# A planned two-layer cross-attention stack: the values in column quarters and 32-row strips, no transposing transfers, the last stage by pairs

## The chip, the cores and the metric

The kernel runs on one core of one Trainium2 chip. The core has five engines with queues of their own: TensorE (PE in the profile; its weight loads stand apart as PEld), VectorE (DVE), ScalarE (ACT), GpSimd (POOL) and SyncE (SP), which here only issues transfers. The metric is the device time of one execution in microseconds; the time before is the median of three runs.

## The reference, cut to what matters

x has 2 x 1024 rows of 256; the context has 2 x 77 rows of 256; 16 heads of 16 features. Four residual stages follow each other, each behind a layer norm:

```python
x = x + tanh(g_xattn[0]) * xattn0(layernorm(x), ctx, ...)        # 16 heads, softmax over 77 keys
x = x + tanh(g_ffn[0])  * ffn0(layernorm(x), w1, w2)             # 256 -> 1024 gelu -> 256
x = x + tanh(g_xattn[1]) * xattn1(layernorm(x), ctx, dist, ...)  # softmax(q k + distance bias), biases
x = x + tanh(g_ffn[1])  * ffn1(layernorm(x), ...)                # expert 0 alone: 256 -> 1024 relu -> 256,
                                                                 # residual, layer norm, gamma, beta
# ffn0, both linears: weights rounded to -1, 0, 1 times their mean magnitude;
# activations rounded to whole numbers of at most 127 in magnitude, by row
```

## The kernel before, in words

The 2048 rows are 16 tiles of 128 rows, in four groups of G = 4. A group runs through four stages: attention of layer 0, `bit_ffn`, attention of layer 1, `expert_ffn`. Nothing is looped on the chip: every step is added to a `Plan` with the tiles that it reads and writes, a cost in microseconds and one or more engines that may do it. `Plan.order` is a list scheduler: of the steps that are ready it takes, engine by engine, the one that can begin first, ties by a weight; buffers of a pool count as resources. `Plan.best` runs it PASSES + 1 times, with weights from the longest path plus `OFFSET[stage][group]` at first and from a backward pass later, and keeps the order with the earliest planned end. `issue` writes it out, so each engine's queue is that order.

**PSUM.** Eight banks: four are the one buffer of scores, `sc` (L711); four are the pool "b" that `bank` hands out for all else. A stage-3 step leaves LEAVE = 2 of them free.

**Attention** (`attention`, L676 on). `norm_group` takes the statistics of the group (`stats`, L517/L518), `inverse_std` makes rstd on POOL (L529, L530) and shift on DVE (L535), and xn = x * rstd + shift is made tile by tile (L553). `transposed_group` turns xn on PE (L581) and evicts it (L371, the line of all evictions by ACT). Queries: L694. Scores: L718, four heads' rows of 32 in four products abreast, 154 keys of two heads each. The softmax of a tile of 128 rows and 8 heads (616 columns) goes: eviction (layer 0, ACT L371) or addition of the distance bias (layer 1, DVE L757); maximum (DVE L766); subtraction (L771); exp (ACT L778); sum (DVE L782) and reciprocal (L787); multiplication (L791). Subtraction and multiplication may go to POOL or DVE; in the order as planned all 64 of each are POOL's. There are 64 such tiles: 2 layers, 4 groups, 2 halves of heads, 4 tiles.

**Values** (`values`, L797 on): for a group and a half of the heads the 616 columns are cut at 128 into five pieces, each turned by four PE transposes (L810) and evicted to pT. A piece crosses heads, so the values stand in `vbd` as blocks of 32 columns (two heads), one for each pair of a piece and a column quarter (`PIECES`, eight of them); `weighted` (L823) runs the eight products of 512 columns in the order of `ORDER`, so that four column quarters run abreast. One eviction brings the sums to OT, and L844 makes the output product.

**bit_ffn** (L978 on). xn is scaled and rounded by adding ROUND (L984), ROUND is taken off again with a bf16 result (`unround`, L963), and a transposing transfer on SP's queue (`turned`, L975) makes xqT. L1007 is the first product, L1015 gelu, then the same rounding (L1023), `unround` to hq, transposing transfer to hqT, second product L1036.

**expert_ffn** (L1053 on). L1071 and L1089 are its two products in f32; L1099 adds the residual, `stats` of all four tiles follow, one `inverse_std`, then gamma and scaling by tile (L1108, L1115), and one store for each tile (L1122).

Transfers are issued from SP in the order of the plan; the four weights of layer 0's attention from ACT.

## Time and profile before

| | us |
|---|---|
| median of 3 runs (385.62 to 386.3) | 385.67 |
| the profiled execution | 384.3 |
| its span, first to last instruction | 382.6 |
| PE busy | 331.5 |
| DVE busy | 279.4 |
| ACT busy | 248.8 |
| POOL busy | 230.9 |

The mean granted TensorE clock was 0.958. The profile's page gives busy sums, the span in 40 slices (each digit a busy share in tenths), the chain of work that ended last, and groups of instructions by line. A busy sum counts a moment once even where instructions overlap; the "mean ns" of a group is the length of one record, which on a pipelined engine can be longer than the spacing of two. A product of f32 operands shows as two records, an f32 transpose as one.

### The profile page before, as it was taken

Reading aid. Unit: us, or ns where it says so; the run is one execution under the profiler, and the core shown is the slowest. Engines: PE = TensorE matmul, PEld = TensorE weight load, DVE = VectorE, ACT = ScalarE, POOL = GpSimd, SP = SyncE. Lnnn points to the kernel's source line nnn. Section 1 sums busy time; section 2 is a strip of 40 time slices with the busy share of each in tenths; the row PEclk is TensorE's granted clock in tenths of the full one; section 3 lists DMA queues with packets and bytes.
Section 4 is the critical chain, followed back from the end, with each engine's and each line's share of the span. In section 5 each row is a group of like instructions: output and inputs, shape, how many; then the busy total and the mean of one; then the engine's idle time right before and its main releaser. Section 6 shows DMA issues by size and latency. Waiting matters only on the chain.

```text
span 382.6 us, 5624 instructions
## 1 busy us (share of the span) xinstructions
PE 331.5 (87%) x1983; PEld 207.2 (54%) x1992; DVE 279.4 (73%) x587; ACT 248.8 (65%) x407; POOL 230.9 (60%) x241
## 2 busy tenths in 40 slices
PE   4883894989758779999899999999999999999991
PEld 3453452446424446644676747446774644785580
DVE  2599889679899997489946899569998994037006
ACT  1797789998788965476629985797556474223300
POOL 6269999631779765489649755313898696025001
PEclk9897998899999788999999999999999999999997
DMA  7972303125011111000100014223000001001001
GB/s 235 337 209 32 110 5 110 32 27 99 1 27 30 28 27 29 0 2 2 29 0 3 0 29 96 69 42 70 2 0 2 1 15 42 0 3 55 0 0 55
DMA packets 39600, 17.73 MB, mean 46 GB/s; under 512 B 30099, under 2 KB 39060, under 8 KB 39572
## 3 DMA queue, kind: packets, MB, share of 16 engines
q1 hardware_dynamic: 38484, 16.33, 16.9%
q10 hardware_dynamic: 1088, 1.05, 0.8%
q8 instruction: 15, 0.25, 0.2%
q14 instruction: 13, 0.11, 0.1%
HBM read 9.71 MB, written 2.10 MB: 31 GB/s over the span
## 4 chain that ended last, share of the span: by engine, by line
PE 45%; DVE 24%; ACT 13%; POOL 9%; issue 4%; DMA 3%; SPq 0%; POOLq 0%; DVEq 0%; ACTq 0%
PE b L1089 10%; PE b L1071 10%; DVE mx L766 5%; PE b L810 5%; PE b L823 5%; PE b L844 5%; POOL probs L791 4%; DVE den L782 4%; PE b L694 4%; DVE probs L757 3%; ACT pT L371 3%; PE b L1036 2%; POOL probs L771 2%; PE sc L718 2%; ACT probs L778 2%
## 5 line engine op out<-in xcount | busy, mean ns | idle before, releaser
L771 POOL TENSOR_TENSOR probs<-probs,mx 128x616 f32<-128x616 f32 x64 | 78.1, 1235 | 34.1 <-DVE mx L766 34.1
L791 POOL TENSOR_TENSOR probs<-probs,den 128x616 f32<-128x616 f32 x64 | 80.9, 1286 | 5.2 <-DVE den L787 4.2
L810 PE MATMUL b<-ident,probs 128*128 128x128 f32 (+1 forms) x320 | 50.1, 300 | 21.7 <-POOL probs L791 9.9
L1089 PE MATMUL b<-staged,hT 128*128 128x256 f32 x256 | 59.2, 382 | 0.0
L1071 PE MATMUL b<-xnT,staged 128*128 128x512 f32 x128 | 57.5, 597 | 0.3 <-ACT xnT L371 0.3
L810 PEld LDWEIGHTS b<-ident,probs 128*128 128x128 f32 (+1 forms) x320 | 37.5, 148 | 37.3 <-POOL probs L791 13.8
L766 DVE TENSOR_REDUCE mx<-probs 128x8 f32<-128x616 f32 x64 | 48.8, 784 | 6.3 <-ACT probs L371 5.7
L1089 PEld LDWEIGHTS b<-staged,hT 128*128 128x128 f32 x256 | 47.5, 190 | 9.4 <-issue 3.4
L778 ACT ACTIVATE probs<-probs 128x616 f32<-128x616 f32 x64 | 44.9, 715 | 11.6 <-POOL probs L771 11.3
L782 DVE TENSOR_REDUCE den<-probs 128x8 f32<-128x616 f32 x64 | 48.8, 767 | 4.6 <-ACT probs L778 4.6
L371 ACT ACTIVATE pT<-b 128x512 f32<-128x512 f32 (+1 forms) x80 | 42.7, 603 | 9.0 <-PE b L810 8.3
L553 ACT ACTIVATE xn<-x,shift,rstd 128x256 f32<-128x256 f32 x64 | 34.0, 595 | 19.4 <-DVE shift L535 19.4
L529 POOL TENSOR_SCALAR rstd<-mv 128x4 f32<-128x4 f32 x20 | 5.4, 268 | 64.0 <-DVE mv L518 63.9
L1071 PEld LDWEIGHTS b<-xnT,staged 128*128 128x128 f32 x128 | 23.5, 190 | 27.1 <-issue 24.7
L371 ACT ACTIVATE hT<-b,eb_sb 128x512 f32<-128x512 f32 x32 | 21.9, 684 | 23.3 <-PE b L1071 23.3
L694 PE MATMUL b<-xnT,wq_sb 128*128 128x512 f32 x64 | 32.8, 634 | 1.2 <-ACT xnT L371 1.2
L823 PE MATMUL b<-pT,vbd 128*32 128x512 f32 (+1 forms) x256 | 31.9, 599 | 1.5 <-ACT pT L371 1.3
L844 PE MATMUL b<-wo_sb,OT 128*128 128x256 f32 x128 | 29.9, 382 | 0.4 <-ACT OT L371 0.3
L517 DVE BATCH_NORM_STATS2 st<-x 128x6 f32<-128x256 f32 x64 | 24.7, 417 | 6.8 <-DMA x<-in_x_dram 5.9
L718 PE MATMUL sc<-kbd,qT 32*128 32x154 f32 x512 | 27.6, 325 | 2.0 <-DVE probs L757 1.3
L718 PEld LDWEIGHTS sc<-kbd,qT 32*128 32x128 f32 x512 | 19.1, 189 | 17.4 <-issue 6.1
L941 DVE TENSOR_REDUCE top_h<-hs 128x1 f32<-128x1024 f32 x16 | 19.3, 1204 | 11.1 <-ACT hs L1015 11.1
(87 smaller groups left out, 491.1 us busy)
## 6 DMA issues: line engine op xcount, KB each, us to landing
x<-in_x_dram SPq DMA_DIRECT2D x16, 128.0 KB
staged<-in_ew_dram SPq DMA_DIRECT2D x2, 1024.0 KB
out_dram<-x SPq DMA_DIRECT2D x16, 128.0 KB
staged<-in_fw1T_dram SPq DMA_DIRECT2D x1, 1024.0 KB
staged<-in_fw2T_dram SPq DMA_DIRECT2D x1, 1024.0 KB
dbias<-in_dist_dram SPq DMA_DIRECT2D x1, 616.0 KB
wk_sb<-in_wkT_dram ACTq DMA_DIRECT2D x1, 256.0 KB
wq_sb<-in_wqT_dram ACTq DMA_DIRECT2D x1, 256.0 KB
```

What stands on the lines that cost most here:

```text
L371: nc.scalar.activation(out(), src(), AF.Relu if relu else AF.Copy if bias is None else AF.Identity, bias=0.0 if bias is None else bias(), ...
L718: nc.tensor.matmul(sc.ap[:, q, j * QK : j * QK + QK], qT.ap[rows, h, at : at + P], kbd.ap[rows, h, b].rearrange("p h s -> p (h s)"), start ...
L766: lambda j, n: nc.vector.tensor_reduce(each(mx, j, n), heads(j, n), AX.X, ALU.max),
L771: lambda e, j, n: e.tensor_tensor(heads(j, n), heads(j, n), bc(each(mx, j, n), 2, SK), ALU.subtract),
L778: lambda j, n: nc.scalar.activation(flat(j, n), flat(j, n), AF.Exp), [pr], [pr],
L782: lambda j, n: nc.vector.tensor_reduce(each(den, j, n), heads(j, n), AX.X, ALU.add),
L791: lambda e, j, n: e.tensor_tensor(heads(j, n), heads(j, n), bc(each(den, j, n), 2, SK), ALU.mult),
L810: lambda j=j, c=c, n=n, tr=tr: nc.tensor.transpose(tr.ap[:n, j, :], prs[j // 2].ap[:, j % 2, c * P : c * P + n], ident.ap),
L823: nc.tensor.matmul(po.ap[32 * q : 32 * q + 32, :], vbd.ap[: CH[c], b, h, s, :], pTs[c].ap[: CH[c], :], start=(i < 4), stop=(i >= 4),)
L844: nc.tensor.matmul(pp.ap[:, j % 2, :], OT.ap[:, k, j * P : (j + 1) * P], wo_sb.ap[:, k, :], start=(k == 0), stop=(k == KT - 1),)
L1071: lambda f=f, k=k, ph=ph: nc.tensor.matmul(ph.ap, ew1_sb.ap[:, k, f * P : (f + 1) * P], xnT.ap[:, k, :], start=(k == 0), stop=(k == KT - 1),),
L1089: lambda j=j, f=f, pp=pp: nc.tensor.matmul(pp.ap[:, j % 2, :], hT[f].ap[:, j * P : (j + 1) * P], ew2_sb.ap[:, f, :], start=(f == 0), stop= ...
```

## The change

Line numbers below are those of the kernel before.

- **Values.** The last 13 of a head's 77 keys are treated apart. The multiplication by the reciprocal is split in two: keys 61 to 76 of each of the 8 heads go to a new strip of 128 columns behind the 616 (written first), keys 0 to 63 are packed to 8 x 64 columns in place. The five transposed pieces are then four of two whole heads each, and the strip. `chunks(i)` makes, for a pair of tiles i, four products of 128 rows, 32 columns, 256 moving columns, one in each column quarter, into a bank of its own; `strips` adds eight products of 32 rows by 32 columns, 256 moving columns. `vbd` is laid out anew, with zeros against the three keys that the strip repeats. OT is evicted by pairs, and the output product of a pair waits for that pair alone. `strip(q, i)` also permutes which bank of `sc` a product of scores goes to.
- **Layer 0 without xn.** x is transposed as it is; Wq is centred once over its 256 inputs (`center`: two products with a matrix of 1/256, one subtraction), and exp takes rstd as its scale for each row. No shift is made for layer 0.
- **No transposing transfers.** Rounding adds LIFT = 0x4400 as well, so that the low half of each f32 is a bf16 pattern; `turned` transposes these halves (stride 2) on PE with a bf16 identity, and one eviction reads PSUM as 16-bit integers, takes LIFT off and writes bf16. `unround`, xq and hq are gone; hs has three buffers for two.
- **Last stage by pairs.** In `expert_ffn` the second pair's second products wait for the first pair's; statistics, rstd and scaling go by pairs, with no shift, and one store serves a pair. Loads of x, from group 1 on, go by pairs too.
- **Planner.** All 16 entries of OFFSET are new, PASSES is 8 for 6, and costs are formulas of the group's size (GROUPS = (4, 4, 4, 4)).

The diff, cut to its core:

```diff
+LIFT = float(0x4400)
+GROUPS = (4, 4, 4, 4)
 OFFSET = (
-    (-5, -26, -123, -47),
-    (-3, -24, -97, -118),
-    (13, 125, -3, -121),
-    (222, 127, -1, 13),
+    (424, -150, -409, -294),
+    (-2, 172, -151, -389),
+    (319, 8, 80, -221),
+    (40, 177, 231, 300),
 )
-PASSES = 6
+PASSES = 8
...
+    MAIN, LAST = 64, 16
+
+    def strip(q, i):
+        return (q + 2 * i) % 4
...
+        def lay(row, part, own, head):
+            parts.append((vbd, len(parts)))
+            n = own.stop - own.start
+            at = slice(HD * head, HD * head + HD)
+            dma(
+                0.5,
+                lambda: nc.sync.dma_start(
+                    out=vbd.ap[row : row + n, part].rearrange("p b k q f -> p (b k q) f")[:, :, at],
+                    in_=v.ap[own].rearrange("p b (q f) -> p (b q) f", f=32)[:, :, at],
+                ),
+                [v], parts[-1:],
+            )
+
+        for head in range(2):
+            lay(MAIN * head, 0, slice(0, MAIN), head)
+        for s in range(4):
+            for head in range(2):
+                lay(32 * s + LAST * head + LAST - (SK - MAIN), 1, slice(MAIN, SK), head)
...
+    def center(w_sb):
+        pm = bank("pm")
+        def mm():
+            for k in range(KT):
+                nc.tensor.matmul(
+                    pm.ap[:, :D], mean.ap, w_sb.ap[:, k, :], start=(k == 0), stop=(k == KT - 1)
+                )
+        pe(0.9, mm, [mean, w_sb], [pm])
+        dve(
+            0.66,
+            lambda: nc.vector.tensor_tensor(
+                w_sb.ap, w_sb.ap, bc(pm.ap[:, :D], 1, KT), ALU.subtract
+            ),
+            [pm, w_sb], [w_sb],
+        )
...
-        xnT = transposed_group(norm_group(g)[1])
+        if layer == 0:
+            xnT = transposed_group(xs[g])
+            rstd = inverse_std(moments.pop(g), n, False)[0]
+        else:
+            xnT = transposed_group(norm_group(g)[1])
...
-            steps(
-                T_MUL, lambda f, r, w, n: by_either(1.22 * n, 0.08 + 0.7 * n, f, r, w),
-                lambda e, j, n: e.tensor_tensor(
-                    heads(j, n), heads(j, n), bc(each(den, j, n), 2, SK), ALU.mult
-                ),
-                [pr, den], [pr],
-            )
+                by_either(
+                    0.44, 0.2,
+                    lambda e, j=j, each=each: e.tensor_tensor(
+                        pr.ap[:, j, HK:].rearrange("p (h s) -> p h s", s=LAST),
+                        heads(j)[:, :, SK - LAST :], each(den, LAST), ALU.mult,
+                    ),
+                    [(pr, j), (den, j)], [(pr, j)],
+                )
+                by_either(
+                    1.03, 0.66,
+                    lambda e, j=j, each=each: e.tensor_tensor(
+                        heads(j, MAIN), heads(j)[:, :, :MAIN], each(den, MAIN), ALU.mult
+                    ),
+                    [(pr, j), (den, j)], [(pr, j)],
+                )
...
-            def weighted():
-                for i, s in enumerate(ORDER):
-                    c, q = PIECES[s]
+            po = [lazy(ps_b, [P, 2 * P], F32, "b", 4, both) for _ in range(2)]
+            def chunks(i):
+                for q in range(4):
                     nc.tensor.matmul(
-                        po.ap[32 * q : 32 * q + 32, :], vbd.ap[: CH[c], b, h, s, :],
-                        pTs[c].ap[: CH[c], :], start=(i < 4), stop=(i >= 4),
+                        po[i].ap[32 * q : 32 * q + 32, :], vbd.ap[:, 0, b, h, q, :],
+                        pTs[strip(q, i)].ap[:, 2 * i * P : 2 * i * P + 2 * P],
+                        start=True, stop=False,
                     )
-            pe(2.0, weighted, vbd_parts + list(pTs.values()), [po])
-            evict(C_512, lambda: OT.ap[:, h, :], lambda: po.ap, [po], [(OT, h)])
+            def strips():
+                for i in range(2):
+                    for q in range(4):
+                        rows = slice(32 * strip(q, i), 32 * strip(q, i) + 32)
+                        nc.tensor.matmul(
+                            po[i].ap[32 * q : 32 * q + 32, :], vbd.ap[rows, 1, b, h, q, :],
+                            pTs[4].ap[rows, 2 * i * P : 2 * i * P + 2 * P],
+                            start=False, stop=True,
+                        )
+            for i in range(2):
+                pe(0.48, lambda i=i: chunks(i), vbd_parts + pTs[:4], [po[i]])
+            pe(0.5, strips, vbd_parts + pTs[4:], po)
...
-    def turned(out, src, n, reads, writes):
-        dma(
-            0.5 + n / 1024, lambda: nc.sync.dma_start_transpose(out=out(), in_=src()), reads, writes
-        )
+    def turned(srcs, out, name, reads_of, writes):
+        n = sum(c for _, c in srcs)
+        tr = bank(name, (P, n, P), BF16)
+        at = 0
+        for (src, c), reads in zip(srcs, reads_of):
+            def mm(src=src, c=c, at=at):
+                for f in range(c):
+                    nc.tensor.transpose(
+                        tr.ap[:, at + f, :], src().bitcast(BF16)[:, 2 * f * P : 2 * (f + 1) * P : 2],
+                        ident_b.ap,
+                    )
+            pe(0.06 * c, mm, [reads, ident_b], [(tr, at), (writes[0], "held")])
+            at += c
+        flat = lambda: tr.ap.rearrange("p c t -> p (c t)").bitcast(I16)
         plan.add(
             [
+                ("ACT", 0.91, lambda: nc.scalar.activation(out(), flat(), AF.Copy, bias=-LIFT)),
...
         for i, t2 in enumerate(both):
+            mv2 = lazy(sm, [P, 2, 2], F32, "mv2", 3)
...
-                        + ([(pp, j - 1)] if j % 2 and f == 0 else []),
+                        [ew2_sb] + hT[f : NF if f == 0 else f + 1] + (before if f == 0 else []),
...
+            r2, _ = inverse_std(mv2, 2, False)
```

## The prediction

> **What bounds the kernel now.** I read the totals and the forty slices first, then the busy time in stretches of 20 us, the chain of waits, the start and one value block in the timeline, and the waits last.
>
> The page (engine totals; slices of 9.6 us):
>
> ```profile
> span 382.6 us, 5624 instructions
> PE 331.5 (87%) x1983; PEld 207.2 (54%) x1992; DVE 279.4 (73%) x587; ACT 248.8 (65%) x407; POOL 230.9 (60%) x241
> PE   4883894989758779999899999999999999999991
> POOL 6269999631779765489649755313898696025001
> ```
>
> Stretches (busy us of each engine, granted clock, DMA share, GB/s):
>
> ```profile
> 20.00:40.00 20.00, 12.87 (x96) 8.36 (x98) 19.73 (x38) 17.66 (x29) 18.00 (x15) 0.83 0.43 105
> 40.00:60.00 20.00, 17.43 (x154) 10.36 (x150) 16.88 (x35) 16.37 (x26) 19.67 (x20) 1.00 0.14 54
> 160.00:180.00 20.00, 20.00 (x97) 9.58 (x96) 16.80 (x36) 12.88 (x23) 16.79 (x16) 1.00 0.00 1
> 340.00:360.00 20.00, 19.75 (x66) 11.42 (x65) 7.00 (x20) 7.46 (x13) 7.73 (x8) 1.00 0.08 26
> ```
>
> PE misses 51 us of the span. Adding up all stretches, 34.9 us of that lie before 140, 8.0 between 140 and 360, 8.2 behind 360. So there are two regimes. Until about 150 the softmax engines set the pace: POOL is busy 37.7 of 40 us from 20 to 60, DVE and ACT about 87% of 20 to 147. From 150 on PE is packed, and a microsecond of PE work is a microsecond of time.
>
> The chain (start, length, what) has a transposing transfer in the early regime, and one in the late:
>
> ```profile
> 37.31 6.59 POOL probs L791 x3
> 72.25 1.90 PE b L823 x16
> 92.09 4.85 DMA hqT<-hq
> 243.88 3.51 DMA xqT<-xq
> ```
>
> The start (timeline; brackets: idle before, and what ended it):
>
> ```profile
> 7.76 0.39 DVE L517 BATCH_NORM_STATS2 st<-x 128x6 f32<-128x256 f32 x1
> 10.29 2.08 ACT L553 ACTIVATE xn<-x,shift,rstd 128x256 f32<-128x256 f32 x4 [2.94 <-DVE shift L535]
> 13.48 4.92 PE L694 MATMUL b<-xnT,wq_sb 128*128 128x512 f32 x8
> 20.80 2.39 POOL L771 TENSOR_TENSOR probs<-probs,mx 128x616 f32<-128x616 f32 x2 [6.96 <-DVE mx L766]
> ```
>
> The fourth tile of x is there at 7.76, but the queries wait until 13.48 for rstd, shift, xn, transposes and an eviction; POOL then sits idle until 20.80.
>
> **The change, part by part.** The sum is made against the profiled execution: 384.3 us, of which 382.6 are its span. The median of the three runs is 385.67, 1.4 above; I carry differences over to the median.
>
> *Values (16 blocks).* A block is 8 products of 32 columns by 512, two records each. Timeline of one block:
>
> ```profile
> 147.45 1.93 PE L823 MATMUL b<-pT,vbd 128*32 128x512 f32 x16
> 149.31 2.42 PE L810 MATMUL b<-ident,probs 128*128 128x128 f32 x20
> ```
>
> From start to next start 1.86 us: four rounds of four records abreast at 0.43, and 0.14 around them. New: 8 products of 256 columns (four rounds at 0.215, 0.86), then 8 of 32 rows by 32 columns. The trace shows four abreast by rows (scores) and four by columns, never both. Eight abreast the strips take two rounds, 0.43; four abreast 0.86. With one more 0.14 for the change of shape a block is 1.57 or 2.00. I take 1.57 (the eight use different rows and columns, as each kind of four does today), rounded to 0.3 saved: 16 x 0.3 = -4.8 us of PE; ends -7 (the extra change free) and +2.2. The eviction to OT splits in two: two of some 0.35 for one of 0.596, +1.7 of ACT in all, beside other work.
>
> The rule against this step: the Trainium skill, TensorEngine Tiling (Array Packing), Key Properties, says that changing the tiling mode drains TensorE. The timeline bounds the changes around today's block at 0.14 in all; the page gives no price, so by it alone the strips could not be costed.
>
> *No transposing transfers.* 24 transfers and 24 un-rounding copies (ACT: 16 at 1.063, 8 at 0.626, 22.0 us) go; 160 transposes of 128 bf16 columns on PE and 20 evictions of 1024 elements come (I take 1.06 each from the hq row, 21.2 us: no change on ACT). A transpose: L1007 streams 512 bf16 columns in 0.215 (four in 0.86 on the chain), so 128 take 0.054; the f32 transposes need 0.117 (20 in 2.35). I take 0.06, nearer the bf16 row: +9.6 of PE, ends +8.6 and +18.7.
>
> The Trainium skill, TensorE: Matmul & The Clock Gate, Part 4, gives about 275 ns for such a transpose in a kernel; 160 would be 44 us and the change a loss. The rows agree with the 275 as the length of a record (L810: 273) and not as the spacing of pipelined ones (0.117), which is what PE pays.
>
> On the path: at 92 the chain pays 4.85 of transfer and 0.95 of hq; instead come 8 x 0.06, a 1.06 eviction and some 0.3 of hand-overs, 1.8. That is -4.0 early. PE waits only 2.4 us for hqT and 0.6 for xqT in all, so the ends are 0 (something else is late next, the softmax's own chain) and -7 (the xqT piece too).
>
> *Layer 0 without xn.* x itself is transposed, Wq is centred once, exp takes rstd as its scale. Gone: 16 xn on ACT (9.5 us), 4 shifts. New: 2 products of 256 columns (0.88), one subtraction (about 0.69 by L1099) and a scale operand in 32 exps, at nothing to 0.1 each (ACT is not the chain early). At the start wv's landing ended a wait at 7.04 and wq was issued ahead of it; 7.04 + 0.88 at up to half clock + 0.69 + hand-overs is about 9.3 for the first query product, not 13.48. All that follows starts 4 us earlier, POOL too, which is free at 13.8: -4.0, ends 0 and -4.2. The subtraction is a new wait on DVE (for PE's means); queued behind it are the statistics of group 1, and rstd of group 1, which the exps want several us later.
>
> *Softmax on POOL.* The 616-element multiplication (1.286) becomes one of 512 and one of 128. Between the rows of 154 elements (0.44) and 616, a straight line gives 1.07 and 0.39: +0.18 a tile. In the POOL-bound stretch 20 to 67 that is 16 tiles: +2.9; but four kbd products of layer 1 (0.44), which stand ahead of the 16th multiplication today, stand behind it in the new order, -1.8. Net +1.1. Ends: in proportion to elements, -1.0; by the 512-element rows L685/L1061 (1.27) plus 0.39, +4.1. Later POOL has 3 us free in 20 and the cost is hidden; if it were not, 48 tiles x 0.18 = 8.6 would show.
>
> *Table loads.* The order has 17 where it had 13: +4 x 1.283 = 5.1 on ACT; with the xn gone ACT comes out about -1 to -3. At nothing, since ACT idles a third; on the chain it would be up to 5.1.
>
> *Last stage by pairs.* The last product ends near 374.4 and the span 8.2 later: addition, statistics, rstd (0.37 + 1.11), four L1115 and the store. By pairs only two tiles follow: two scalings fewer (1.0), but gamma's step now queues behind rstd (+0.5): -0.4. Four more rstd pairs on POOL (1.35 each) fall where it is free. On SP's queue 8 stores stand for 16, 10 loads of x for 16, 20 copies into vbd for 24 (0.83 each by L664) and no transposes (1.2 each): it is through earlier, and its waits are for others anyway, so nothing.
>
> *Late regime.* In the new order 80 of the 160 transposes and 8 of 16 blocks stand behind the middle of the softmax tiles: 80 x 0.06 - 8 x 0.3 = +2.4, ends +0.8 and +10.5. Expert products fill gaps there: the new order has them in 45 runs where it had 30, and 126 of the 192 ahead of the last softmax transpose where it had 112. I take 3 of the 8 us of idle back: -3, ends 0 and -5.
>
> *Order before 150.* OFFSET is new in all 16 entries, so the planner orders everything afresh. DVE works 111 of the 126 us from 20 to 146; no order gains more than 15 there. I take 0, ends -10 and +8.
>
> Sum: -4.0 - 4.0 + 1.1 - 0.4 + 2.4 - 3.0 + 0 = -7.9 us. Profiled execution 376.4, median 377.8.
>
> **The rivals.**
>
> *The order fills the early gaps (faster still).* For it: 34.9 us of PE idle before 140, no engine full over that whole stretch. Against it: POOL at 94% from 20 to 60, with more work per tile. With the order's -10: 367.8.
>
> *PE gets heavier.* Strips four abreast and transposes at 0.117: late 80 x 0.117 + 8 x 0.14 = +10.5 for +2.4. For it: neither is in the trace. Against it: the bf16 row. It gives 385.9, and with the waits hidden anyway 390.
>
> *Banks (ends slower).* Four PSUM banks serve everything but the scores. Each block now needs two at once for its sums, and 20 turned tiles hold one from transposes to eviction (0.5 + 1.06 + 0.3). Where PE meets a full pool it waits for an eviction, 0.60 by the pT row. The waits show the seed:
>
> ```profile
> PE b L810 <- ACT pT L371: 5.2, 8, 2.1
> PE b L1007 <- ACT pT L371: 3.2, 3, 2.1
> ```
>
> 36 places x 0.60 = 21.6, on top of -7.9: 399. It decides from 0.22 a place. Against it: the planner counts banks, and these two add up to 8.4 in the whole run.
>
> *The transfers were hidden and so was the start.* Only +1.1 + 2.4 - 0.4 - 3.0 remain: 385.8, no change.
>
> **How the numbers follow.** Forecast 0.47 (372 to 384); order 0.26 (362 to 372); heavier PE 0.12 (385 to 393); banks 0.10 (388 to 400); hidden 0.05 (385 to 387). Leaving out the lowest and highest tenth: 365 to 391. This kernel's measurement tells about 0.2% from no change, 384.9 to 386.4. Faster: 0.47 + 0.26 and 0.03 from the edges of the others; same 0.05; slower 0.19.
>
> **What would show it.** First query product before 10 us and first POOL subtraction near 17 (start). Value blocks at 1.5 to 1.6 start to start, turned transposes near 0.06 apart. No DMA in the chain after the loads. POOL's two products summing to 1.46. PE idle before 140 near 27. Wrong if PE's waits for evictions exceed 15 us, or PE's busy sum passes 345.

## The result and the profile after

The changed kernel takes 383.67 us (median of 10 executions, 382.04 to 384.77), the kernel before 385.68 beside it (10 executions): a ratio of 0.9944, with a 95% interval of 0.9928 to 0.9961. That is 2 us faster, where the prediction said 7.9. The profiled execution took 382.45 us, of which 380.7 are its span (before: 384.3 and 382.6).

The page of the changed kernel, engine totals and two rows of slices:

```profile
span 380.7 us, 6452 instructions
...
PE 341.6 (90%) x2412; PEld 220.1 (58%) x2412; DVE 279.1 (73%) x580; ACT 250.8 (66%) x407; POOL 252.0 (66%) x316
...
PE   5967798699698899999999798999989999999991
...
POOL 6489999885875886499759864396505689326011
```

PE is busy 10.1 us more and POOL 21.1 more; POOL's second to fourth slices read 489 where they read 269. The start, from the timeline:

```profile
8.60 1.79 PE L711 MATMUL b<-wq_sb,mean 128*128 128x256 f32 x4
...
10.50 0.69 DVE L718 TENSOR_TENSOR wq_sb<-wq_sb,b 128x512 f32<-128x512 f32 x1 [2.25 <-PE b L711]
...
11.33 2.81 PE L749 MATMUL b<-xnT,wq_sb 128*128 128x512 f32 x6
...
16.54 2.40 POOL L819 TENSOR_TENSOR probs<-probs,mx 128x616 f32<-128x616 f32 x2 [2.17 <-DVE mx L814]
```

The first query product moved from 13.48 to 11.33, the first subtraction on POOL from 20.80 to 16.54. Stretches of 20 us (columns as before):

```profile
20.00:40.00 20.00, 14.00 (x106) 7.99 (x102) 19.48 (x40) 19.03 (x30) 19.79 (x23) 0.83 0.51 98
40.00:60.00 20.00, 16.66 (x149) 10.94 (x140) 18.82 (x38) 15.12 (x24) 19.52 (x20) 0.83 0.33 106
...
200.00:220.00 20.00, 17.33 (x136) 13.62 (x135) 19.02 (x36) 17.71 (x28) 18.04 (x23) 1.00 0.00 0
220.00:240.00 20.00, 18.74 (x162) 10.23 (x159) 9.22 (x25) 11.38 (x23) 9.75 (x10) 1.00 0.08 28
```

POOL, now the last of five columns of busy time, is full from 20 to 60 (19.8 and 19.5; before 18.0 and 19.7). PE is short of 3.9 us between 200 and 240. PE's timeline there shows what for:

```profile
211.88 1.46 PE L1179 MATMUL b<-staged,hT 128*128 128x256 f32 x6
214.34 1.08 PE L1094 MATMUL b<-fw_q,xqT 128*128 128x512 bf16 x4 [1.00 <-ACT hqT L1059]
215.26 0.60 PE L872 MATMUL b<-ident,probs 128*128 128x128 f32 x4
217.53 0.61 PE L1049 MATMUL b<-ident_b,hs 128*128 128x128 bf16 x8 [1.67 <-ACT hs L1102]
```

The expert products of a group (L1179) run out at 213.3, and for 4 us PE has only pieces of `bit_ffn` and of a softmax, each as late as DVE and ACT make it. The wait that ends at 217.53 is for gelu (L1102), and ACT's timeline has a table load just ahead of it:

```profile
214.67 0.81 ACT L826 ACTIVATE probs<-probs,rstd 128x616 f32<-128x616 f32 x1
215.50 1.28 ACT L1102 ACT_TABLE_LOAD   x1
216.79 1.27 ACT L1102 ACTIVATE hs<-b,down_x 128x512 f32<-128x512 f32 x2
```

The chain of waits (start, length, what) runs over DVE up to there, with the scalings of `bit_ffn` and the softmax's reductions taking turns, and then over these two:

```profile
206.88 1.36 DVE hs L1110
208.24 1.14 DVE top_h L1020
209.79 0.75 DVE hs L1110
210.54 1.40 DVE mx L814 x2
...
215.51 1.27 ACT L1102
216.79 0.70 ACT hs L1102
217.53 0.61 PE b L1049 x8
```

To account for the span I cut it where PE ends the 160th of the 320 f32 transposes of probs ("middle"); about there the softmax stops setting the pace. "Late" is from the middle to the end of PE's last product, "behind PE's end" what follows it. All in us, from the profiled executions:

| | middle | late PE busy | late PE idle | late, sum | behind PE's end | span |
|---|---|---|---|---|---|---|
| before | 151.7 | 216.4 | 6.3 | 222.7 | 8.2 | 382.6 |
| after | 146.4 | 220.4 | 6.2 | 226.6 | 7.7 | 380.7 |
| forecast for after | -6.9 | +2.4 | -3.0 | -0.6 | -0.4 | -7.9 |
| measured | -5.3 | +4.0 | -0.1 | +3.9 | -0.5 | -1.9 |

The early gain came, nearly as forecast. The late stretch, forecast a little shorter, became 3.9 longer.

### The profile page after: what moved, and what is told of

Read it like the earlier page. It is cut to its first block, busy times and chain, and to the rows that moved or that the text cites. A ratio compares the mean times of both kernels' runs of the same rounds, so it can differ in the third digit from the quotient of the medians.

```text
span 380.7 us, 6452 instructions
## 1 busy us (share of the span) xinstructions
PE 341.6 (90%) x2412; PEld 220.1 (58%) x2412; DVE 279.1 (73%) x580; ACT 250.8 (66%) x407; POOL 252.0 (66%) x316
## 3 DMA queue, kind: packets, MB, share of 16 engines
q10 hardware_dynamic: 1088, 1.05, 0.8%
## 4 chain that ended last, share of the span: by engine, by line
PE 54%; DVE 28%; ACT 7%; POOL 6%; issue 2%; DMA 1%; POOLq 0%; DVEq 0%
PE b L1179 12%; PE b L1160 12%; PE b L923 5%; PE b L749 5%; PE b L872 4%; DVE mx L814 4%; PE sc L773 3%; DVE top_h L1020 3%; DVE den L834 3%; PE b L884 3%; PE b L601 3%; DVE hs L1110 2%; POOL probs L851 2%; PE b L1094 2%; DVE st L534 2%
## 5 line engine op out<-in xcount | busy, mean ns | idle before, releaser
L851 POOL TENSOR_TENSOR probs<-probs,den 128x512 f32<-128x512 f32 x64 | 68.3, 1074 | 2.6
L872 PE MATMUL b<-ident,probs 128*128 128x128 f32 x320 | 52.1, 302 | 13.1 <-POOL probs L851 6.2
L1179 PE MATMUL b<-staged,hT 128*128 128x256 f32 x256 | 61.0, 383 | 0.0
L872 PEld LDWEIGHTS b<-ident,probs 128*128 128x128 f32 x320 | 39.4, 153 | 30.2 <-POOL probs L851 11.1
L372 ACT ACTIVATE pT<-b 128x512 f32<-128x512 f32 x80 | 44.0, 600 | 16.0 <-PE b L872 15.5
L1179 PEld LDWEIGHTS b<-staged,hT 128*128 128x128 f32 x256 | 47.0, 190 | 8.8 <-issue 2.5
L546 POOL TENSOR_SCALAR rstd<-mv 128x4 f32<-128x4 f32 (+1 forms) x24 | 6.9, 287 | 62.3 <-DVE mv L535 56.7
L572 ACT ACTIVATE xn<-x,shift,rstd 128x256 f32<-128x256 f32 x48 | 25.2, 591 | 17.8 <-DVE shift L553 17.8
L803 DVE TENSOR_TENSOR probs<-sc,dbias 128x616 f32<-128x616 f32 x32 | 24.7, 788 | 13.8 <-PE sc L773 13.7
L1189 DVE TENSOR_TENSOR xn<-b,xn 128x512 f32<-128x512 f32 x8 | 5.4, 681 | 39.5 <-PE b L1179 36.7
L843 POOL TENSOR_TENSOR probs<-probs,den 128x128 f32<-128x128 f32 x64 | 27.2, 433 | 7.6 <-DVE den L838 5.5
L826 ACT ACTIVATE probs<-probs,rstd 128x616 f32<-128x616 f32 x32 | 25.1, 806 | 5.5 <-POOL probs L819 5.4
```

The costliest lines, as they stand in the source:

```text
L372: nc.scalar.activation(out(), src(), AF.Relu if relu else AF.Copy if bias is None else AF.Identity, bias=0.0 if bias is None else bias(), ...
L851: lambda e, j=j, each=each: e.tensor_tensor(heads(j, MAIN), heads(j)[:, :, :MAIN], each(den, MAIN), ALU.mult),
L872: lambda j=j, at=at, tr=tr: nc.tensor.transpose(tr.ap[:, j, :], prs[j // 2].ap[:, j % 2, at : at + P], ident.ap),
L1179: lambda j=j, f=f, pp=pp: nc.tensor.matmul(pp.ap[:, j % 2, :], hT[f].ap[:, j * P : (j + 1) * P], ew2_sb.ap[:, f, :], start=(f == 0), stop= ...
```

## The experiments

Every run shared a chip with runs of the kernel before; times below are its ratio times 385.67, so that runs from different chips can be compared. On that scale the changed kernel is 383.5. The expectations were written on the medians of their chips, about 0.6 lower (382.9).

### Where does a microsecond of work count?

`p_turn2` makes every 16-bit transpose twice:

```diff
-                for f in range(c):
+                for f in [f for f in range(c) for _ in range(2)]:
```

> The changed kernel in its own order, with each of the 160 bf16 transposes on PE made twice (the second writes the same values): 160 x 0.067 = 10.7 us more of PE work, half of it behind the middle of the softmax tiles. Theory of the two regimes (PE is packed from about 146 us on, and what it does before that is hidden behind the softmax engines): the late half counts, +4.8, and little of the early half, so +5 (4 to 8) against the changed kernel, 388 to 391. Rival, every PE microsecond counts wherever it stands: +10.7, 394. Rival, the written order and its waits set the time and PE has room: +0 to +2, 384 to 386.

`p_nostrips` leaves the strip products out (the last 13 keys of each head are missing from the sums):

```diff
-            pe(0.5, strips, vbd_parts + pTs[4:], po)
+            pe(0.5, lambda: None, vbd_parts + pTs[4:], po)
```

> The changed kernel in its own order without the 128 products of 32 rows (the last 13 keys of each head are left out of the values): PE loses 9.6 us by its row, 5.3 of it behind the middle. Two regimes: -5.3 late and 0 to -2 early, 376 to 379. Every PE microsecond counts: -9.6, 374. PE has room: -2 to 0.

`p_nolast` leaves out POOL's 64 multiplications of the strip (the fifth transpose reads other columns, which carry no meaning):

```diff
-                    lambda e, j=j, each=each: e.tensor_tensor(
-                        pr.ap[:, j, HK:].rearrange("p (h s) -> p h s", s=LAST),
-                        heads(j)[:, :, SK - LAST :], each(den, LAST), ALU.mult,
-                    ),
+                    lambda e: None,
```

> The changed kernel in its own order without POOL's 64 multiplications of 128 columns (the strip is transposed from the unscaled probabilities; the other products are as they were): POOL loses 64 x 0.413 = 26.5 us, nothing else changes. If POOL sets the pace from 20 to 60 us, the 16 tiles there give 16 x 0.413 = 6.6 at most, and I expect -3 to -6, all before the middle; late nothing. If POOL's busy stretch is only one of three engines that run close to each other, -2 to 0.

The order of the work is the changed kernel's in all three.

| | time | ratio, interval | middle | late, sum |
|---|---|---|---|---|
| after | 383.5 | 0.9944 (0.9928 to 0.9961) | 146.4 | 226.6 |
| p_turn2 | 387.8 | 1.0054 (1.0038 to 1.0070) | 147.4 | 230.2 |
| p_nostrips | 380.4 | 0.9862 (0.9846 to 0.9878) | 147.0 | 223.0 |
| p_nolast | 377.8 | 0.9795 (0.9780 to 0.9810) | 141.0 | 225.9 |

The 160 transposes take 10.75 us of PE in the changed kernel (start to next start). Twice as many cost 4.3 in all, +1.0 early and +3.6 late, where half of them (4.8 us) lie. The strips' 9.6 us are worth 3.1, all of it late, where 5.3 us of them lie. So PE's work is nearly free early and paid late, as the prediction had it, but late at two thirds to three quarters of its length (3.55 of 5.3 and 3.6 of 4.8), not in full: without the strips PE's late idle grew from 6.2 to 8.2. POOL is the mirror image: 26.4 us of POOL's work are worth 5.7, 5.4 of them early. Half of that work, 13.2 us, lies early, so 0.41 of each early microsecond of POOL is on the path. The clock granted to PE before the middle was higher in `p_nolast` too (0.93 for 0.88), and PE's early work 5.0 us shorter. That can account for about 1 of the 5.4 at most, since `p_turn2` gave PE some 6 us more early and paid 1.0.

### How much does the order decide?

`o_after_mid` is the changed kernel with its 16 OFFSET entries moved by about 10 each; of 59 such draws the one with the median planned end (the end time of the planner's own schedule, by its costs).

> The changed kernel with its 16 entries of OFFSET moved by about 10 each, the median by planned end of 59 such draws (planned 385.5 where the kernel as it is has 367.4); every instruction is the same but for its place. Order theory (the chip follows the plan): 10 to 18 us slower, 394 to 402. If the planned end of an order says little about the chip: within 4 us of 383.7.

It took 400.8 (1.0393, 1.0373 to 1.0412): middle 156.0, late 235.3, of which 15.3 PE idle. This order costs more than all parts of the change together were to gain. That raised the question whether the changed kernel's own order was a good one. `o_after2` and `o_after3` are the changed kernel in orders of a search of mine over OFFSET, `o_before2` and `o_before3` the kernel before in other orders:

```diff
 OFFSET = (
-    (424, -150, -409, -294),
-    (-2, 172, -151, -389),
-    (319, 8, 80, -221),
-    (40, 177, 231, 300),
+    (-15, -31, -438, -46),
+    (3, -28, -949, -602),
+    (31, 102, -92, 121),
+    (177, 261, -326, 417),
 )
```

(this is `o_after3`; the others differ in these 16 numbers alone)

> The changed kernel with another order alone: OFFSET from a search of my own that did not start from the changed kernel's values (planned end 368.0 for 367.4, planned late idle of PE 3.5 for 5.9, planned middle 2.2 later). If the planner's end is good to within a microsecond, 383.5. If orders of like planned ends scatter on the chip, it lies anywhere from 379 to 387, and the distance to 382.9 is a measure of how far one order can speak for a part.

> The changed kernel with a third order near the run o_after2's (planned end 367.2, 0.2 below the changed kernel's own; planned late idle of PE 4.3). If what o_after2 gained (-5) is that PE doesn't wait late (its late idle is 2.1 for 6.2), this one lies between, 377 to 381. If o_after2 was a lucky draw, it lies at 382.9 plus or minus 4.

> The kernel before with another order alone (OFFSET from the same search that gave the run o_after2; planned end 375.9 for its own 373.7, planned middle 6 us earlier, planned late idle of PE 10.6 for 3.8). If the change's parts are worth what my prediction gave them (about -8) and its own order hides it, the kernel before can't be brought near 377.6 by an order: 384 to 392. If an order alone is worth as much for the kernel before as it was for the changed one (-5), 380, and the parts are then worth 2 to 3 us and no more.

> The kernel before with a third order (all 16 entries of OFFSET moved by about 10, the best of 59 such draws by planned end: 374.6 for its own 373.7; planned late idle of PE 5.3 for 3.8, planned middle 7.9 later). If the kernel before has an order on the chip that is as much better as the changed kernel's were (-5.6), it may show here: 380. If not, 384 to 391, like the run o_before2 (389.4).

| | planned end | time | ratio, interval | middle | late PE busy | late PE idle | span |
|---|---|---|---|---|---|---|---|
| before | 373.7 | 385.7 | 1 | 151.7 | 216.4 | 6.3 | 382.6 |
| o_before2 | 375.9 | 389.6 | 1.0102 (1.0064 to 1.0140) | 144.3 | 222.3 | 11.8 | 386.5 |
| o_before3 | 374.6 | 386.2 | 1.0013 (0.9987 to 1.0040) | 160.6 | 210.6 | 5.8 | 385.2 |
| after | 367.4 | 383.5 | 0.9944 (0.9928 to 0.9961) | 146.4 | 220.4 | 6.2 | 380.7 |
| o_after2 | 368.0 | 378.0 | 0.9800 (0.9764 to 0.9836) | 146.5 | 220.7 | 2.1 | 377.0 |
| o_after3 | 367.2 | 378.0 | 0.9800 (0.9778 to 0.9821) | 144.2 | 221.4 | 2.3 | 375.6 |

This shows where the gain went. The changed program in another order is 7.7 us faster than before, about what the prediction gave its parts. That the two numbers agree is in part luck: the profiled execution of `o_after2` is 5.6 shorter than that of the kernel before, from middle -5.2, late work +4.3, late idle -4.2 and -0.5 behind PE's end, where the prediction had -6.9, +2.4, -3.0 and -0.4. Against the changed kernel as it stands, `o_after2` has the same middle and nearly the same late work on PE, and 4.1 us less late idle. The profiled executions of the two lie 3.7 apart, which that idle covers; the rest of the 5.5 between their times is not located. The kernel before got nothing from two other orders. That is the weaker half of the comparison: these two were planned 2.2 and 0.9 later than its own order, while `o_after2` and `o_after3` were planned level with the changed kernel's, and two orders don't exclude a better one. In `o_after3` the stretch where the changed kernel starved reads:

```profile
200.00:220.00 20.00, 19.75 (x151) 15.47 (x153) 19.27 (x46) 19.88 (x33) 18.15 (x25) 1.00 0.00 1
220.00:240.00 20.00, 19.79 (x132) 12.71 (x125) 15.22 (x40) 12.38 (x20) 7.11 (x10) 1.00 0.08 27
```

DVE and POOL are as busy from 200 to 220 as they were (19.3 for 19.0, 18.2 for 18.0), but PE works 19.75 for 17.33: it still has other products to fill in. The planned end doesn't show this: it is 367.4, 368.0 and 367.2 for the three orders of the changed kernel, within 0.8 of each other, and the chip put 5.5 between them. The plan's own late idle of PE does show it: 5.9, 3.5 and 4.3 in the expectations, 6.2, 2.1 and 2.3 on the chip.

### What is each part worth?

Each of three runs puts one part back as it was and has an order of its own from the same search (`u_values` and `u_values3`: the values; `u_dmat`: transposing transfers and un-rounding; `u_xn0`: layer 0's xn). The core of the shortest:

```diff
-        if layer == 0:
-            xnT = transposed_group(xs[g])
-            rstd = inverse_std(moments.pop(g), n, False)[0]
-        else:
-            xnT = transposed_group(norm_group(g)[1])
+        xnT = transposed_group(norm_group(g)[1])
...
-    center(wq0_sb)
```

> The changed kernel with only the values part put back as before (one multiplication of 616 columns, pieces that cross heads, eight products of 512 columns, one eviction), and a new order from the same planner, searched over OFFSET (planned end 373.3, where the changed kernel has 367.4). By the planner this part is worth 5.9 us, so about 389.6. By what the three earlier fixed-order runs showed it is worth little: putting it back costs PE late about 16 x 0.2 = 3 us and gives POOL back 0.2 us a tile, which at the rate of the run without strip multiplications (5.7 us for 0.41 a tile) is -2.7 us early, so 383 to 385. A result near 383 to 386 speaks for the second, 388 or more for the first.

> The changed kernel with the values part put back, with another order (planned end 372.8 for 373.3). With its first order it took 380.0. If the values part is a loss of POOL's time early, near 380 again, above the changed kernel's best order (377.6) and below its own (382.9); with a scatter of orders of 5 us nothing more than 375 to 385 can be said.

> The changed kernel with only the transposing transfers put back (24 transfers, 24 un-rounding copies, no transposes of 16-bit halves), order searched anew (planned end 369.5, 2.1 above the changed kernel). My prediction's step said -4.0 early for the change and +4.8 late (80 transposes at 0.06), net +0.8: undone about 382.9. By the planner 385.7. If the late transposes are a pure loss, as the run with every one of them made twice says (+3.6 late), this kernel's late stretch should be 3 to 5 us shorter than the changed kernel's 226.6, and its middle (160th of the softmax transposes) 3 to 5 us later than 146.4.

> The changed kernel with layer 0's normalised x put back (xn on ScalarE, shift, no centring of Wq, exp without its scale), order searched anew (planned end 377.3, 9.9 above the changed kernel). My prediction's step: 4.0 us, all of it at the start; 387.7. By the planner 393.5. First query product back from 11.3 to 13 or later, first subtraction on POOL back from 16.5 to about 20.5, and the middle of the softmax transposes 4 to 8 us later than 146.4.

| | time | ratio, interval | PE busy | PE idle before its end | middle |
|---|---|---|---|---|---|
| after | 383.5 | 0.9944 | 341.6 | 31.5 | 146.4 |
| o_after3 | 378.0 | 0.9800 | 338.9 | 29.0 | 144.2 |
| u_values | 381.2 | 0.9883 (0.9856 to 0.9910) | 340.5 | 31.8 | 135.7 |
| u_values3 | 380.3 | 0.9861 (0.9834 to 0.9888) | 341.5 | 31.0 | 136.6 |
| u_dmat | 383.5 | 0.9944 (0.9921 to 0.9967) | 330.9 | 42.1 | 143.1 |
| u_xn0 | 389.2 | 1.0091 (1.0057 to 1.0124) | 343.0 | 35.7 | 152.4 |

Two readings of the values part are possible. Against the changed kernel's own order, putting it back gains 2 to 3 us; against the orders that suit the new program, the part is worth 2 to 3. The second compares searched with searched, and I hold to it; with a scatter of several us between orders its size is not firm. (The middles of `u_values` and `u_values3` come from their slowest executions, 1.8 and 2.8 above the medians.) The transfers show a plain exchange in PE's totals: with them PE works 10.7 us less than in the changed kernel, about what the 160 transposes take, and stands idle 11 to 13 more than in the two kernels above. Late, `u_dmat` has 8.5 us of that idle. Its time is that of the changed kernel in its own order and 5.5 above the two better ones, so by searched against searched the part is worth its place, with one order as evidence and not in the way I costed it: the middle of `u_dmat`, 143.1, is not later than that of the kernels without transfers. Layer 0's xn costs 5.7 against the changed kernel's own order, 11.2 against the better ones, and moves the middle by 6 to 8. The three do not add up to the whole, since each has one or two orders only.

### A version without the split

`v_inter` interleaves the two heads of a column quarter, so that one multiplication of 616 on POOL serves again and nothing is packed; the last 32 columns of each quarter are turned by a product with the identity into a quarter of their own:

```diff
-        kbd = lazy(cp, [P, KT, B, 2, SK], F32, f"kbd{layer}", 1)
+        kbd = lazy(cp, [P, KT, B, SK, 2], F32, f"kbd{layer}", 1)
...
+                        for q in range(4):
+                            nc.tensor.matmul(
+                                tr.ap[32 * q : 32 * q + 32, j, :],
+                                pr[:, QK * q + QK - 32 : QK * q + QK], ident.ap,
+                                start=True, stop=True,
+                            )
```

> A version made to use what the runs showed: the two heads of a column quarter stand interleaved (key 0 of both, key 1 of both, ...), so that keys 0 to 63 of both are 128 columns in a row and the last 16 of both 32 columns in a row, with no packing and no strip. The softmax has one multiplication of 616 on POOL (as before the change, 1.25) in place of 1.04 + 0.41; the strip's piece is turned by four products of 32 columns with the identity. Order searched anew (planned end 369.2, 1.8 above the changed kernel). If POOL sets the early pace, as the run without the strip multiplications says (5.7 us for 0.41 us a tile), 0.2 us a tile is worth about -2.8 us: 380.5; the order, which the planner puts 1.8 us worse, gives 382 to 383. If the access by twos is slower on DVE or POOL than a straight row (maxima and sums read every second element), it is slower: 0.1 us on each of 64 x 2 reductions is up to +6, 388.

It took 389.2 (1.0091, 1.0066 to 1.0116). The groups (busy us, mean ns of one, then idle before):

```profile
L844 POOL TENSOR_TENSOR probs<-probs,den 128x616 f32<-128x616 f32 x64 | 78.2, 1248 | 7.5 <-DVE den L839 7.2 <-DVE top_h L1028 0.2
L817 DVE TENSOR_REDUCE mx<-probs 128x8 f32<-128x616 f32 x64 | 48.9, 783 | 3.8 <-ACT probs L372 3.0
L866 PE MATMUL b<-ident,probs 128*32 128x128 f32 x512 | 19.4, 286 | 2.1 <-DVE x L1131 1.1 <-ACT pT L372 0.9
```

Access by twos costs nothing in the reductions (783 ns for the maximum, as before, and 762 for the sum, where it was 765), so that reason falls. The multiplication (1248 ns) doesn't test it: it still walks neighbouring elements, and only its factor alternates between two heads. What the version adds is on PE: the four quarters of a strip take 0.28 us a tile (512 records, 35 ns each up to the next start) in place of 0.14 for one transpose counted the same way, some 9 us in all, 5 of them late. That accounts for about 5 of the 11 us by which it is slower than `o_after3`. Another 5 lie early (its middle is 149.4 for 144.2), though POOL has less to do; that part was not taken apart, and its order is one draw.

### DVE's passes that hold POOL

In the changed kernel four POOL instructions between 39 and 50 us take 0.98 longer than their like, each beside one of DVE's four passes over 2048 columns of the feed-forward's weights. One such pair, and one of POOL's beside a reduction, DVE above, POOL below:

```profile
45.02 2.11 DVE L985 TENSOR_SCALAR staged<-staged,rs 128x2048 f32<-128x2048 f32 x1
...
50.52 0.78 DVE L814 TENSOR_REDUCE mx<-probs 128x8 f32<-128x616 f32 x1
```

```profile
44.99 1.05 POOL L851 TENSOR_TENSOR probs<-probs,den 128x512 f32<-128x512 f32 x1
46.00 2.20 POOL L819 TENSOR_TENSOR probs<-probs,mx 128x616 f32<-128x616 f32 x1
...
50.64 1.22 POOL L819 TENSOR_TENSOR probs<-probs,mx 128x616 f32<-128x616 f32 x1
```

`p_port` gives those passes a second tensor operand (a column of constants, repeated along the row), in the same order of work:

```diff
-                lambda w_f=w_f, rs=rs: nc.vector.tensor_scalar(
-                    w_f(), w_f(), rs.ap, 1.0, ALU.mult, ALU.min
+                lambda w_f=w_f, rs=rs: nc.vector.scalar_tensor_tensor(
+                    w_f(), w_f(), rs.ap, every(4), ALU.mult, ALU.min
```

> The changed kernel in its own order; only the four passes over the 2048-column weights of the feed-forward (L985, L992) are written with two tensor operands instead of one, so the arithmetic is the same. In the changed kernel these four take 2.25, 2.12, 2.02 and 1.45 us on DVE, and just the four POOL instructions that run beside them take 0.97 us longer than their like (2.20 for 1.22 twice, 2.02 for 1.05, 1.39 for 0.41). If it is the one-operand form on DVE that holds POOL up, those four POOL instructions fall back to 1.22, 1.05 and 0.41, and since POOL sets the pace there (19.8 and 19.5 us busy of 20 from 20 to 60), the time falls by 2 to 4 us, to 379 to 381. If it is any long instruction of DVE, nothing changes (382.9).

It was the other way round: 388.7 (1.0079, 1.0054 to 1.0104), 5.2 slower. The timeline of `p_port`, POOL above, DVE below:

```profile
43.02 3.09 POOL L856 TENSOR_TENSOR probs<-probs,den 128x512 f32<-128x512 f32 x1
...
47.89 1.05 POOL L856 TENSOR_TENSOR probs<-probs,den 128x512 f32<-128x512 f32 x1
48.89 3.26 POOL L824 TENSOR_TENSOR probs<-probs,mx 128x616 f32<-128x616 f32 x1
...
55.66 1.22 POOL L824 TENSOR_TENSOR probs<-probs,mx 128x616 f32<-128x616 f32 x1
```

```profile
42.02 3.19 DVE L997 SCALAR_TENSOR_TENSOR staged<-staged,minus_half 128x2048 f32<-128x2048 f32 x1
...
47.92 3.17 DVE L990 SCALAR_TENSOR_TENSOR staged<-staged,rs,minus_half 128x2048 f32<-128x2048 f32 x1
```

A POOL instruction beside such a pass takes 2.04 us longer (3.26 for 1.22), with the one-operand form 0.98 (2.20 for 1.22). DVE's records hold a wait as well: the pass at 47.92 ends at 51.09, 2.15 after POOL's instruction before it (47.89 + 1.05 = 48.94), and in the changed kernel the pass at 45.02 ends 1.09 after POOL's (44.99 + 1.05 = 46.04). Read so, the pass waits for POOL's instruction in flight, and POOL then stands still for nearly as long as the pass itself lasts. A reduction of DVE beside POOL shows no such thing (1.22 at 50.64). The Trainium skill has the rule (SBUF — State Buffer, Who interferes with whom): DVE and GpSimd share a pair of ports, held for a whole instruction, taken by `tensor_scalar` in its two-port modes and by DVE instructions with two inputs from SBUF (against one of GpSimd that reads SBUF), and never by `tensor_reduce`; my expectation had the second of these wrong, and the run agrees with the page.

In the profiled executions all of the loss falls early: the middle is 153.8 for 146.4 (that execution was 1.7 slower than the median), the late stretch 226.5 for 226.6. Before the middle POOL is busy 4.2 us more and DVE 3.2, since the two-operand passes are longer on DVE too; the run doesn't separate the two. `u_port` is the same edit on `u_values`, `u_cal` the same program planned with costs nearer to the trace:

> The kernel with the values part put back (380.0), in the same order, with the same four passes over the weights in the two-operand form. If the passes cost POOL 0.97 us each there too, 376 to 378; otherwise 380.

> The same program as the run u_port, step for step, but planned with costs nearer the trace (the values block 1.86 for 2.0, the four passes over the weights 2.25 for 1.26, the subtraction 1.225 for 1.2, the two scalings of the feed-forward 0.65 and 0.83 for 0.50 and 0.76, the centring product 1.8 for 0.9) and OFFSET searched anew. If a better priced plan is worth anything it beats the run u_port by 1 to 4 us (373 to 377); if orders scatter by as much as the planner's errors, it may lie 4 us on either side of it.

They took 385.0 (0.9982, 0.9964 to 1.0000) and 387.0 (1.0035, 0.9999 to 1.0072). The first is 3.8 slower than `u_values`, as `p_port` would have it. The second varies more than the others (mostly near 384.4 or near 388.7) and is not faster than the first: correcting a handful of costs did not by itself give a better order. `v_clip` goes the other way and shortens the passes: one over f32, ScalarE's copy to bf16, then the clip on the copy.

```diff
                 lambda w_f=w_f, rs=rs: nc.vector.tensor_scalar(
-                    w_f(), w_f(), rs.ap, 1.0, ALU.mult, ALU.min
+                    w_f(), w_f(), rs.ap, ROUND, ALU.mult, ALU.add
...
+                lambda wq_f=wq_f: nc.vector.tensor_scalar(
+                    wq_f(), wq_f(), 1.0, -1.0, ALU.min, ALU.max
```

> The changed kernel with the rounding of the feed-forward's weights shortened: one pass on DVE over 2048 f32 columns (scaled, rounded), ScalarE's copy to bf16, then the clip on the bf16 copy, in place of two f32 passes and the copy. Order searched anew (planned end 368.3, late idle 3.4). POOL is held for the length of each such pass (0.98 us beside the one-operand form, 2.05 beside the two-operand form, where the run p_port lost 5.2 us for 4.3 us more of it): two passes of 0.98 fewer, two of 0.3 to 0.5 more, so about 1 to 1.4 us less on POOL and 1.3 less on DVE early. Against the run o_after2, whose plan it resembles: 1 to 3 us, 375 to 377, if the orders are alike on the chip.

```profile
40.39 0.68 DVE L999 TENSOR_SCALAR fw_q<-fw_q 128x2048 bf16<-128x2048 bf16 x1
...
41.73 1.24 DVE L999 TENSOR_SCALAR fw_q<-fw_q 128x2048 bf16<-128x2048 bf16 x1
```

The clip on bf16 takes 0.68 in the shorter of its two passes. The whole took 377.3 (0.9784, 0.9763 to 0.9806), the fastest of all, late idle 1.4. That it beats `o_after3` by 0.7 lies within both intervals, so the gain of the shorter passes is not shown by it; that the changed program, here with this edit, has orders some 8 us below the kernel before is shown a third time.

## Why the prediction was wrong, and where right

**The two regimes: right in the main.** PE's work counts late, POOL's early (`p_turn2`, `p_nostrips`, `p_nolast`). "A microsecond of PE work is a microsecond of time" is too strong: it is two thirds to three quarters. The forecast's signs for the early half mostly came: first subtraction on POOL at 16.54 (near 17), PE's idle time before 140 us at 25.0 (near 27), no transfer in the chain after the loads. None of its signs looked at PE's late idle.

**Start, -4.0: right in size, wrong in one stage.** POOL's first subtraction came 4.26 earlier. The first query product was put at 9.3 and came at 11.33: the centring products started at 8.60, not 7.04, and took 1.79, twice the 0.88 costed at full pace, though the clock granted from 8 to 10 was 1.00; no run shows why. The scores followed the queries closely enough to make it good. Taking xn back (`u_xn0`) moved the middle 6 to 8 later.

**Transfers, -4.0 early: not confirmed.** The middle moved by 5.3 where start, transfers and POOL together were to give 6.9. With the start at -4.3 and POOL at the +2.6 of the next paragraph, -3.6 is left over, which would fit; but the new order is in that remainder too, and with the transfers put back the middle is not later (143.1). Their price shows as PE's idle time over the whole run, 8.5 us of it late.

**POOL, +1.1: too small, by an estimate.** The two products take 1.45 us a tile for 1.25 (each up to the next start), +0.20. The forecast had +0.18; its own straight line through 0.44 and 1.286 gives 1.10, not 1.07, for the larger one, and so +0.20 too. It counted 16 tiles in full, less 1.8 for four kbd products that move behind the 16th multiplication. They did move, to 87 to 113 us, but that is still ahead of the middle, so the 1.8 is no gain there. By `p_nolast` 0.41 of POOL's early time is on the path, on 32 tiles: +0.20 x 32 x 0.41 = +2.6. The difference of 1.5 is about the whole early error of 1.6.

**PE's prices: right.** A value block takes 1.59 us from start to end of its strips (1.57 forecast), the strips 0.59, less than the 0.86 that the forecast had for four abreast:

```profile
190.40 1.07 PE L884 MATMUL b<-pT,vbd 128*32 128x256 f32 x16
191.40 0.66 PE L894 MATMUL b<-pT,vbd 32*32 32x256 f32 x16
191.99 0.70 PE L1179 MATMUL b<-staged,hT 128*128 128x256 f32 x2
```

16-bit transposes lie 0.056 apart within a run and cost 0.067 each over all (0.06 forecast). So the rules that were weighed did not decide: the change of tiling costs about the 0.14 a block allowed for (0.16), and the 275 ns of the Trainium skill (TensorE: Matmul & The Clock Gate, Part 4) come near the length of a record (219 to 251 ns here) and are not the spacing. Of +2.4 late for these two, 4.8 - 3.0 = +1.8 came (nine value blocks lie late, not eight).

**Late idle taken back, -3.0: this step failed.** It was 6.3 and is 6.2. The prediction counted the expert products ahead of the last softmax transpose, and in how many runs they were spread, and took that for cover. The counts don't tell: in the traces all three orders of the changed program have 126 of them ahead, in 37 or 38 runs, with a late idle of 6.2, 2.1 and 2.3. What counts is whether any are left when DVE and ACT are late; at 213 us they had run out, and 3.9 of the 6.2 us of idle follow by 232. The plan itself had PE's late idle at 5.9, where the kernel before is planned with 3.8, so it pointed the other way. Beside it, two query products more lie behind the middle (28 records for 24, +2.2 us), which the sum left out. These two, less the 0.6 by which the values saved more than forecast, give the late error: 2.9 + 2.2 - 0.6 = 4.5 of the 6.0 us by which the sum was off; 1.6 are early, and behind PE's end 0.1 came back.

**Order, 0 with ends -10 and +8: it looked at the wrong stretch.** The term was for the order before 150, and 0 was a guess. There the other three orders of the changed program differ from its own by -2.2 to +9.6 (middles 144.2 to 156.0); most of what the order gave away against `o_after2` lies behind, as late idle. The gain of the parts is there (378.0 in two other orders); the order that came with them gave 5.5 of it away.

**Table loads, at nothing: nearly right.** There are 17, as planned. Six of them are in the chain where five were, 7.7 us for 6.1, and one stands in the stretch above where PE starved (215.51).

**The rivals.** Heavier PE falls by the prices above. Banks: the largest of PE's waits for evictions by ACT read

```profile
PE b L1049 <- ACT OT L372: 2.0, 1, 2.0
PE b L872 <- ACT OT L372: 1.8, 1, 1.8
PE b L872 <- ACT qT L372: 1.7, 2, 1.1
```

With pT (1.3, 1.3 and 1.2) they add up to 9.3 us; with the smaller rows and the waits for hqT, xqT and xnT, some of which PE needs as data, to 13.4. That is under the 15 that the prediction had set as its mark and far from 21.6. That the change was hidden gives 385.8 for the 383.7 measured, but its reason falls, since the middle moved by 5.3. The range of 365 to 391 held the result and both good orders, but not the median draw.

## What to carry to other kernels

When a change comes with a new order of the work, the parts and the order are two changes: cost the order by the stretches in which the busiest engine may starve, and ask what product is left to fill each, not how many there are in all. If a planner writes the order, read its idle time of the busiest engine late in the plan, not its end alone, and try two or three orders that it calls equal before judging a part; here they lay 5.5 us apart on the chip, more than the change as it was made. Split a POOL instruction only where POOL has slack: 0.41 of its early time came out at the end.

## What the runs showed of the hardware

- A DVE pass over SBUF with one f32 tensor operand (2048 columns) held POOL's instruction beside it for 0.98 us, with two operands for 2.04; beside a reduction POOL kept its 1.22.
- DVE's reductions over every second f32 took as long as those over neighbours (maximum 783 ns in both, sum 762 for 765).
- Products of 32 rows and 32 columns run more than four abreast: 8 products of 256 columns in f32 took 0.59 us, where four abreast would need 0.86 by the rounds of the value block before (0.43 for four records of 512).
- The f32 product with the identity in four column quarters is dearer than one f32 transpose of 128 columns: 0.28 us for 0.14, each up to the next start.
- With a scale from a column of SBUF, exp over 616 columns took 806 ns, without one 715.
